# Corner weights of a bilinear gather: a multiply with broadcast weights and two pair sums on VectorE, in place of scale and accumulate tap by tap on two engines

## The chip, the cores and the metric

The kernel runs on one core of one Trainium2 chip. The metric is the device time of one launch in microseconds (us). The core has five engines with queues of their own: PE (TensorE), DVE (VectorE), ACT (ScalarE), POOL (GpSimd) and SP (SyncE). Each runs its instructions in the order in which the program put them. SP issues plain DMAs; POOL issues the indirect ones, which gather rows of a DRAM tensor by a list of indices.

## The reference

Four layers run over four samples of 96 channels and 128 x 128 pixels, all in float32, each layer added to its input. Layer 2 is a deformable 3 x 3 convolution, and only its sampling is touched here:

```python
offset = _conv(x, offset_w, offset_b)
mask = jax.nn.sigmoid(_conv(x, mask_w, mask_b))
...
for k in range(K * K):
    i, j = (k // K, k % K)
    dy = offset[:, 2 * k]
    dx = offset[:, 2 * k + 1]
    py = base_y[None, :, None] + i * DIL + dy
    px = base_x[None, None, :] + j * DIL + dx
    samp = _bilinear(x, py, px) * mask[:, k][:, None]
    out = out + jnp.einsum('bchw,oc->bohw', samp, weight[:, :, i, j])
```

`_bilinear` takes, for every pixel, the four corners around (py, px) and adds them with the weights (1-wy)(1-wx), (1-wy)wx, wy(1-wx) and wy wx. So every pixel and each of the nine taps has four weights (here already multiplied by the mask) and four vectors of 96 channels, and the sample is the weighted sum of the four vectors. The other layers are a selective scan along the pixels (layer 0), convolutions with two-dimensional transforms (layer 1), and a transform, a large selective scan with 16 states and the inverse transform (layer 3).

## The kernel before

**Stages and lanes.** The samples overlap. First the front of sample 0 runs (layers 0 and 1 and the preparation of layer 2). Then for each sample b there is a stage with two lanes side by side: the "back" of sample b (the gather of layer 2, then the head and the forward transform of layer 3), and the front of sample b+1 with the inverse transform of sample b-1. After it come the scans of layer 3 of sample b, by themselves. For the last sample there is no next front; the lane beside it has only the inverse transform of the sample before, which is done early, so that most of that gather runs alone. There are four gathers: three beside a front, one alone.

**Order.** Inside a two-lane stage the program is recorded first: a planner (`Program`, line 238) keeps a cost per operation (`cost`, line 368), measures each lane once for due times, and issues the operations of both lanes engine by engine, by the earliest start and then by the due time. `InOrder` (line 56) keeps that order on the chip. All instructions of these stages are issued at line 66, a helper, so groups are told apart by their tiles. A tile's name stands in the profile without digits: `l2_g` is `l_g`, `l2_sm` is `l_sm`, `l2_v` (the weights) is `l_v`.

**The data.** `offsets` (line 1247) writes three DRAM tensors: `quad_d`, which holds for each pixel the 4 x 96 values of its four corners; `idx_d`, the row of `quad_d` for each pixel and tap; and `w4_d`, the four weights for each pixel and tap. On its way it runs DVE operations on tiles `l_off`, `l_p`, `l_rd`, `l_w`. The front lane's layer 0 runs the scan `l_h` on DVE with its products `l_du` on POOL and `l_ct` on DVE.

**The gather** (`gather`, line 1421) goes row by row over the 128 rows of the image; partition w holds pixel w of the row. For a row, POOL issues nine indirect DMAs, one a tap, each of 128 rows of 384 floats, into the tile `l2_g` [128, 9, 384]. There are four such tiles beside the other lane, six in the last stage (`room`, line 1410). In the turns of the next row, `weigh(row, 0)` is recorded for taps 0 to 4 and `weigh(row, 1)` for taps 5 to 8; both read the weights from `l2_v`. For each tap ACT scales corner 0 into `l2_sm` and corner 2 into `l2_part`; DVE adds corner 1 times its weight to the first and corner 3 times its weight to the second. One DVE sum for each half then adds `l2_part` to `l2_sm`. A row's `l2_sm` [128, 9, 96] is then transposed by PE (`turn`), copied to SBUF by ACT (`keep`) and multiplied with the convolution's weights by PE (`finish`). Every four rows DVE adds bias and input (`l_x<-l_pc`) and takes statistics.

Of the kernel before, what the change touches and what calls it, by code (L numbers as in the profile page):

```python
# [23 lines left out]
F32 = mybir.dt.float32  # L24
F32R = mybir.dt.float32r
I32 = mybir.dt.int32
AF = mybir.ActivationFunctionType
ALU = mybir.AluOpType
# [4 lines left out]
C, H, W = 96, 128, 128  # L33
# [492 lines left out]
class Net:  # L526
# [894 lines left out]
    def gather(self, T, wp, wb, ps, rows, sums, kept, lag, slack):  # L1421

        nc, a = self.nc, self.a
        T.x3, T.st3 = self.plane("x3"), self.stats_tile()
        KC = 7

        wk = wp.tile([128, KC, C], F32, name="l2_wk")
        for k in range(9):
            c = 0
            while c < C:  # L1430
                at = k * C + c
                n = min(C - c, 128 - at % 128)
                nc.sync.dma_start(
                    out=wk[at % 128 : at % 128 + n, at // 128, :], in_=a["l2_wT"][c : c + n, k, :]
                )
                c += n
        bk = self.load(wp, a["l2_b"], [C, 1], "l2_bk")
        gts, sms, work = {}, {}, {}

        def fetch(g):  # L1440
            idx = wb.tile([128, 36], I32, name="l2_i", tag="i", bufs=3)
            nc.sync.dma_start(out=idx, in_=T.idx_d[:, 36 * g : 36 * (g + 1)])
            w4 = wb.tile([128, 144], F32, name="l2_v", tag="v", bufs=3)
            nc.sync.dma_start(out=w4, in_=T.w4_d[:, 144 * g : 144 * (g + 1)])
            xc = self.load(wb, T.x2[:, g * CH : (g + 1) * CH], [C, CH], "l2_x", 3)
            work[g] = SimpleNamespace(idx=idx, w4=w4, xc=xc)

        def weigh(row, m):


            if m == 0:
                sms[row] = wb.tile([128, 9, C], F32, name="l2_sm", tag="sm", bufs=sums)
            taps = slice(5 * m, 5 + 4 * m)
            part = wb.tile([128, 5, C], F32, name="l2_part", tag="part")
            sm = sms[row][:, taps]
            g4 = gts[row][:, taps].rearrange("p k (q c) -> p k q c", c=C)
            for k in range(5 - m):
                at = 36 * (row % 4) + 4 * (5 * m + k)
                w = [work[row // 4].w4[:, at + q : at + q + 1] for q in range(4)]
                for q, out in ((0, sm), (2, part)):  # L1460
                    nc.scalar.activation(out[:, k, :], g4[:, k, q, :], AF.Copy, scale=w[q])
                    nc.vector.scalar_tensor_tensor(
                        out[:, k, :], g4[:, k, q + 1, :], w[q + 1], out[:, k, :], ALU.mult, ALU.add
                    )
            nc.vector.tensor_tensor(sm, sm, part[:, : 5 - m], ALU.add)

        def turn(p, c):
            v = units[p, c] = SimpleNamespace(ks=[k for k in (2 * c, 2 * c + 1) if k < KC])
            v.pt = ps.tile([128, 2, 2, W], F32, name="l2_pt2", tag="t")
            for i, k in enumerate(v.ks):  # L1470
                n = min(128, 9 * C - 128 * k)
                for r in range(2):
                    flat = sms[2 * p + r].rearrange("p k c -> p (k c)")
                    nc.tensor.transpose(v.pt[:n, i, r, :], flat[:, 128 * k : 128 * k + n], self.ident)

        def keep(p, c):
            v = units[p, c]
            v.sT = wb.tile([128, 2, 2, W], F32, name="l2_sT", tag="sT", bufs=kept)
            n = min(128, 9 * C - 128 * v.ks[-1])
            nc.scalar.copy(v.sT[:n, : len(v.ks)], v.pt[:n, : len(v.ks)])  # L1480

        def finish(p, c):
            g, h = divmod(p, 2)
            w, v = work[g], units.pop((p, c))
            if h == 0 and c == 0:
                w.pc = ps.tile([128, CH], F32, name="l2_pc", tag="pc", bufs=1)[:C]
            for i, k in enumerate(v.ks):
                n = min(128, 9 * C - 128 * k)
                nc.tensor.matmul(
                    out=w.pc[:, 2 * W * h : 2 * W * (h + 1)], lhsT=wk[:n, k, :],  # L1490
                    rhs=v.sT[:n, i].rearrange("c r w -> c (r w)"),
                    start=k == 0, stop=k == KC - 1,
                )
            if h == 1 and c == 3:
                nc.vector.scalar_tensor_tensor(w.xc, w.pc, bk, w.xc, ALU.add, ALU.add)
                nc.vector.bn_stats(T.st3[:, g, :], w.xc)
                nc.sync.dma_start(out=T.x3[:, g * CH : (g + 1) * CH], in_=w.xc)

        fetch(0)
        units = {}  # L1500
        self.program.slack = slack
        at = (0, 4, 9, 13)
        for row in range(H + 6):
            if row % 4 == 2 and row // 4 + 1 < H // 4:
                fetch(row // 4 + 1)
            for k in range(9):
                if row < H:
                    if k == 0:
                        gts[row] = wb.tile([128, 9, 4 * C], F32, name="l2_g", tag="g", bufs=rows)
                    i = (row % 4) * 9 + k  # L1510
                    nc.gpsimd.indirect_dma_start(
                        out=gts[row][:, k, :],
                        out_offset=None,
                        in_=T.quad_d[:],
                        in_offset=work[row // 4].idx[:, i : i + 1],
                    )
                if k in (2, 5) and 0 <= row - 1 < H:
                    weigh(row - 1, k // 5)
                for late, step in ((0, turn), (lag, keep), (lag + 4, finish)):
                    p, m = divmod(9 * row + k - 27 - late, 18)  # L1520
                    if 0 <= p < H // 2 and m in at:
                        step(p, at.index(m))
                yield
        self.program.slack = 0.0
# [926 lines left out]
```

## Time and profile before

Median 14923.91 us of 3 runs (14919.98 to 14983.37). The profiled execution took 14956.1 us, and its span from the first to the last instruction is 14954.0 us.

| stretch, us from the start | what runs | POOL busy of it |
|---|---|---|
| 0 to 1318 | front of sample 0 | |
| 1318 to 3190 | gather of sample 0, beside front of sample 1 | 1270.70 |
| 4817 to 6676 | gather of sample 1, beside front of sample 2 | 1270.59 |
| 8345 to 10195 | gather of sample 2, beside front of sample 3 | 1264.33 |
| 11826 to 13292 | gather of sample 3, most of it alone | 1114.65 |
| between and behind | layer 3's head, transform and scans of each sample | |

Each gather issues 1152 indirect DMAs. A line of the profile's groups reads: line, engine, operation, out<-in by tiles, partitions x elements, count | busy us, mean ns of one | idle time of the engine just before them and what ended most of it. "issue" is time in which the engine waited for nothing that the profile shows. Lines in order of time read: start, us, engine, line, operation, tiles, [idle before <- what ended it].

### The profile page before, as it was taken

Reading aid. Unit: us, or ns where it says so; the run is one execution under the profiler, and the core shown is the slowest. Engines: PE = TensorE matmul, PEld = TensorE weight load, DVE = VectorE, ACT = ScalarE, POOL = GpSimd, SP = SyncE. Lnnn points to the kernel's source line nnn. Section 1 sums busy time; section 2 is a strip of 40 time slices with the busy share of each in tenths; the row PEclk is TensorE's granted clock in tenths of the full one; section 3 lists DMA queues with packets and bytes.
Section 4 is the critical chain, followed back from the end, with each engine's and each line's share of the span. In section 5 each row is a group of like instructions: output and inputs, shape, how many; then the busy total and the mean of one; then the engine's idle time right before and its main releaser. Section 6 shows DMA issues by size and latency. Waiting matters only on the chain. (4 is left out here: it accounts for less than half of the span.)

```text
span 14954.0 us, 175601 instructions
## 1 busy us (share of the span) xinstructions
PE 12275.2 (82%) x48112; PEld 5769.1 (39%) x48112; DVE 11311.0 (76%) x21823; ACT 8881.9 (59%) x21508; POOL 10357.0 (69%) x7904
## 2 busy tenths in 40 slices
PE   7897787879998978878999878887999744459998
PEld 3353344343333434443333334534333422233334
DVE  4625686678998587677999678667999765558997
ACT  3614675556665586555666467555666465546664
POOL 2103747748998755765999774774999877758997
PEclk9998898979999988978999989888999855569999
DMA  6445658766666758875666766876666755556676
GB/s 163 135 131 187 185 168 249 233 205 177 188 196 192 243 169 225 236 221 162 194 189 193 222 202 176 255 237 186 192 189 196 213 171 168 166 153 184 187 199 193
DMA packets 1313229, 2890.16 MB, mean 193 GB/s; under 512 B 281008, under 2 KB 767600, under 8 KB 1197936
## 3 DMA queue, kind: packets, MB, share of 16 engines
q1 hardware_dynamic: 1013872, 1972.56, 45.8%
q0 software_dynamic: 298368, 906.38, 20.5%
q8 instruction: 381, 6.24, 0.2%
q14 instruction: 608, 4.98, 0.1%
HBM read 2455.55 MB, written 422.58 MB: 192 GB/s over the span
## 5 line engine op out<-in xcount | busy, mean ns | idle before, releaser
L66 POOL DMA_INDIRECT l_g<-quad_d,l_i x4608 | 4664.4, 1012 | 2516.9 <-issue 1330.6
L66 POOL TENSOR_TENSOR l_hc<-l_h,l_cl 128x1024 f32<-128x1024 f32 x1536 | 3608.5, 2361 | 288.6 <-DVE l_h L66 264.1
L66 PE MATMUL l_py<-l_hc,ident 128*128 128x512 f32 x6144 | 3073.9, 611 | 181.2 <-POOL l_hc L66 177.9
L66 DVE TENSOR_TENSOR_SCAN l_h<-l_dA,l_carry,l_dB 128x512 f32<-128x512 f32 x2304 | 2861.4, 1265 | 1.7
L66 ACT ACTIVATE l_dA<-l_dl,l_al 128x512 f32<-128x512 f32 x2304 | 1637.4, 718 | 1111.6 <-DVE l_h L66 1102.6
L66 DVE SCALAR_TENSOR_TENSOR l_sm<-l_g,l_v,l_sm 128x96 f32<-128x96 f32 x4608 | 1480.5, 322 | 1039.4 <-ACT l_sm L66 1004.6
L66 ACT ACTIVATE l_sm<-l_g,l_v 128x96 f32<-128x96 f32 x4608 | 1680.1, 369 | 646.8 <-DMA l_g<-quad_d,l_i 612.3
L66 ACT ACTIVATE l_part<-l_g,l_v 128x96 f32<-128x96 f32 x4608 | 1656.6, 364 | 213.3 <-DVE l_sm L66 213.1
L66 PEld LDWEIGHTS l_py<-l_hc,ident 128*128 128x128 f32 x6144 | 1135.2, 192 | 1348.3 <-issue 828.0
L66 PE MATMUL l_pc<-l_sT,l_wk 128*96 128x256 f32 (+1 forms) x3584 | 1238.3, 470 | 449.9 <-ACT l_sT L66 447.4
L66 DVE TENSOR_TENSOR l_dB<-l_du,l_pB 128x512 f32<-128x512 f32 x2304 | 1492.2, 677 | 48.7 <-POOL l_du L66 27.7
L66 PE MATMUL l_pB<-l_bc,pick 128*128 128x512 f32 x2304 | 1402.1, 637 | 136.1 <-DVE l_dB L66 122.1
L66 DVE SCALAR_TENSOR_TENSOR l_part<-l_g,l_v,l_part 128x96 f32<-128x96 f32 x4608 | 1477.8, 321 | 43.8 <-ACT l_part L66 43.1
L66 PE MATMUL l_pt<-ident,l_sm 128*128 128x128 f32 (+1 forms) x3584 | 793.7, 326 | 750.7 <-DVE l_sm L66 746.2
L66 POOL TENSOR_TENSOR l_dP<-l_du,l_cl 128x512 f32<-128x512 f32 x768 | 978.1, 1274 | 100.9 <-DMA l_cl<-bc_d 71.6
L66 DVE TENSOR_TENSOR_SCAN l_h<-l_dQ,l_carry,l_dP 128x512 f32<-128x512 f32 x768 | 971.1, 1264 | 58.1 <-POOL l_dP L66 54.7
L66 PEld LDWEIGHTS l_pc<-l_sT,l_wk 128*96 128x96 f32 (+1 forms) x3584 | 643.2, 199 | 962.4 <-ACT l_sT L66 552.2
L66 PEld LDWEIGHTS l_pt<-ident,l_sm 128*128 128x128 f32 (+1 forms) x3584 | 521.7, 164 | 1140.1 <-DVE l_sm L66 874.7
L66 ACT COPY l_sT<-l_pt 128x512 f32<-128x512 f32 (+1 forms) x1024 | 522.3, 522 | 626.8 <-PE l_pt L66 625.5
L66 POOL TENSOR_TENSOR l_du<-l_du,l_dl 96x512 f32<-96x512 f32 x256 | 339.9, 1328 | 792.8 <-DVE l_dl L66 482.5
L66 PE MATMUL l_pc<-rows,l_wc 96*32 96x508 f32 (+3 forms) x6912 | 841.7, 612 | 46.7 <-DVE rows L66 46.7
L66 PEld LDWEIGHTS l_pB<-l_bc,pick 128*128 128x128 f32 x2304 | 438.5, 191 | 1062.2 <-DVE l_dB L66 834.5
(274 smaller groups left out, 19887.2 us busy)
## 6 DMA issues: line engine op xcount, KB each, us to landing
l_cl<-bc_d SPq DMA_DIRECT2D x512, 1280.0 KB
l_cl<-bc_d SPq DMA_DIRECT2D x512, 640.0 KB
quad_d<-l_qt SPq DMA_DIRECT2D x124, 768.0 KB
l_g<-quad_d,l_i POOLq DMA_INDIRECT x4608
x<-l_x SPq DMA_DIRECT2D x352, 192.0 KB
l_uc<-u_d SPq DMA_DIRECT2D x256, 192.0 KB
l_x<-x SPq DMA_DIRECT2D x224, 192.0 KB
l_xs<-x SPq DMA_DIRECT2D x116, 256.0 KB
```

The lines of the kernel that those rows point to most:

```text
L66: ins = op(*args, **kw).ins
```

## The change

`weigh` weighs a half row at once. One DVE operation multiplies the gathered tile in place, all taps of the half, four corners and 96 channels (128 x 1920 or 128 x 1536 elements), by the weights, each of which is repeated over 96 channels by a stride of zero. A second adds the last two corners to the first two (128 x 960 or 128 x 768), in place too. A third adds the two halves of that into `l2_sm` (128 x 480 or 128 x 384). ACT has no part in it any more, and the tile `l2_part` is gone. The indirect DMAs, their tiles and the number of these, the transposes and the rest are written as before; the planner works out the order of the stage anew from the new operations.

```diff
             taps = slice(5 * m, 5 + 4 * m)
-            part = wb.tile([128, 5, C], F32, name="l2_part", tag="part")
-            sm = sms[row][:, taps]
-            g4 = gts[row][:, taps].rearrange("p k (q c) -> p k q c", c=C)
-            for k in range(5 - m):
-                at = 36 * (row % 4) + 4 * (5 * m + k)
-                w = [work[row // 4].w4[:, at + q : at + q + 1] for q in range(4)]
-                for q, out in ((0, sm), (2, part)):
-                    nc.scalar.activation(out[:, k, :], g4[:, k, q, :], AF.Copy, scale=w[q])
-                    nc.vector.scalar_tensor_tensor(
-                        out[:, k, :], g4[:, k, q + 1, :], w[q + 1], out[:, k, :], ALU.mult, ALU.add
-                    )
-            nc.vector.tensor_tensor(sm, sm, part[:, : 5 - m], ALU.add)
+            n = 5 - m
+            at = 36 * (row % 4) + 20 * m
+            w = work[row // 4].w4[:, at : at + 4 * n].rearrange("p (k q) -> p k q", q=4)
+            g4 = gts[row][:, taps]
+            by_q = g4.rearrange("p k (q c) -> p k q c", c=C)
+            nc.vector.tensor_tensor(by_q, by_q, w.unsqueeze(3).to_broadcast([128, n, 4, C]), ALU.mult)
+            nc.vector.tensor_tensor(g4[:, :, : 2 * C], g4[:, :, : 2 * C], g4[:, :, 2 * C :], ALU.add)
+            nc.vector.tensor_tensor(sms[row][:, taps], g4[:, :, :C], g4[:, :, C : 2 * C], ALU.add)
```

## The prediction

> **What bounds the kernel now.** I read the page first, then the busy times by stretch, then the groups of single engines inside stretches, then the order of time at a few places.
>
> The page, first two lines of part 1 and the first of part 5:
>
> ```profile
> span 14954.0 us, 175601 instructions
> PE 12275.2 (82%) x48112; PEld 5769.1 (39%) x48112; DVE 11311.0 (76%) x21823; ACT 8881.9 (59%) x21508; POOL 10357.0 (69%) x7904
> L66 POOL DMA_INDIRECT l_g<-quad_d,l_i x4608 | 4664.4, 1012 | 2516.9 <-issue 1330.6
> ```
>
> No engine is full, since the span is a row of stages with different limits. Busy time by stretch (time, then PE, PEld, DVE, ACT, POOL, each with its count, then the clock, the DMA share and GB/s) shows three kinds: a gather beside the other lane, the gather of the last sample alone, and the layer-3 scans.
>
> ```profile
> 2500.00:2750.00 250.00, 193.57 (x1322) 96.06 (x1326) 142.65 (x463) 127.73 (x446) 183.86 (x188) 0.90 0.76 222
> 4250.00:4500.00 250.00, 238.51 (x600) 97.20 (x599) 244.00 (x269) 172.88 (x325) 237.16 (x132) 1.00 0.69 197
> 12250.00:12500.00 250.00, 107.67 (x308) 65.94 (x308) 148.53 (x452) 142.67 (x440) 189.98 (x198) 0.56 0.57 166
> ```
>
> The change touches the first and third kind. In both POOL does little but indirect DMAs, at nearly one rate. POOL's groups from 12000 to 13250 us, and from 2260 to 3190 us (count, then busy, mean ns, idle before it):
>
> ```profile
> L66 POOL DMA_INDIRECT l_g<-quad_d,l_i x985 | 951.2, 966 | 300.1 <-issue 279.4 <-DVE l_sm L66 12.5 <-DVE l_part L66 6.4
> ...
> L66 POOL DMA_INDIRECT l_g<-quad_d,l_i x675 | 685.3, 1015 | 244.2 <-issue 184.6 <-DVE l_part L66 41.1 <-DMA l_g<-quad_d,l_i 11.5
> ```
>
> An undisturbed one takes 0.946 us (the median) and the next starts 0.304 us later: 1.25 us each, 11.25 us for a row of nine. Alone, 985 fill the 1250 us (1.27 each); beside the other lane 675 fill 930 (1.38). So the gather stages are set by how fast POOL can issue gathers. The exception is the layer-0 scan inside each of the first three stages (1740 to 2260 us and its like), where POOL waits for DVE. The same group in the other five stretches outside it counts 304, 333, 679, 316 and 690; with the 675 that is 2997 DMAs or 333 rows. The last stage has 128 rows, the three layer-0 stretches 51.
>
> What lengthens a DMA is seen in the order of time (start, us, engine):
>
> ```profile
> 10048.24 0.84 DVE L66 TENSOR_TENSOR l_off<-l_ot 128x656 f32<-128x656 f32 x1
> 10048.33 1.56 POOL L66 DMA_INDIRECT l_g<-quad_d,l_i  x1 [0.30 <-DVE l_ot L66]
> 10049.11 0.84 DVE L66 TENSOR_TENSOR l_off<-l_off,l_ot 128x656 f32<-128x656 f32 x1
> ...
> 9054.46 1.27 DVE L66 TENSOR_TENSOR_SCAN l_h<-l_dA,l_e,l_du 96x512 f32<-96x512 f32 x1
> 9054.64 2.49 POOL L66 DMA_INDIRECT l_g<-quad_d,l_i  x1 [0.30 <-issue]
> 9055.65 0.66 DVE L66 TENSOR_TENSOR l_ct<-l_ct,l_z 96x512 f32<-96x512 f32 x1
> ```
>
> The first began inside a DVE operation with both inputs in SBUF and ended 0.82 us after that operation (49.90 against 49.08), though a second one, dependent on the first, ran from 0.03 us later. The second sat through a scan and an independent product that followed without a gap, and ended 0.82 us after the product (57.13 against 56.31). So a gather passes one point, 0.946 - 0.82 = 0.13 us after its start, only while no such DVE operation runs; the 0.03 us gap before a dependent operation lets it through. The 96-element operations of before are too short to matter: 0.966 against 0.946.
>
> **The change part by part.** *Removed:* ACT's 2 x 4608 scalings (1680.1 + 1656.6 us) and DVE's 9216 accumulations and 1024 sums (1480.5 + 1477.8 + 637.1 = 3595 us, 7.02 a row). ACT's 6.5 us a row hid beside POOL's 11.4, so it is worth nothing by itself. *Added:* six DVE operations a row, all with two SBUF inputs. Their durations come from the same operation at two widths alone, with one broadcast row as a check:
>
> ```profile
> L66 DVE TENSOR_TENSOR l_sm<-l_sm,l_part 128x480 f32<-128x480 f32 x112 | 73.7, 658 | 3.8
> L66 DVE TENSOR_TENSOR l_sm<-l_sm,l_part 128x384 f32<-128x384 f32 x113 | 63.0, 558 | 3.9
> ...
> L66 DVE TENSOR_TENSOR pick<-ident 128x768 fp32r<-128x768 f32 x8 | 7.2, 943 | 0.0
> ```
>
> 96 more elements cost 100 ns, so 1.042 each on 158. Products of 1920 and 1536: 2.158 and 1.758 us; sums of 960, 480, 768 and 384: 1.158, 0.658, 0.958, 0.558. Together 7.25 us a row. The row of 768, whose inputs are both broadcast in the innermost place, took 0.943 where this gives 0.958: repeating an element is not slow. The upper bound is the four-apart write, l_w<-l_w,l_w at 144 elements, 0.503 us: (503 - 158)/144 = 2.4 ns each; the lower is 1.042. I take the lower. DVE's own sum is then +0.2 us a row, hidden under POOL.
>
> The product waits for all of its five or four taps where ACT began with each, so the sums, the transposes on PE behind them and the release of the gather's buffer come later, by up to the 3.97 or 3.27 us of a half's three operations. Alone PE works 656.95 of 1464 us (11826 to 13290) and has the room; a buffer is wanted again six rows on, or four beside the other lane, 45 us at 11.4 a row. I cost it at nothing; were that cover gone, POOL would wait 3 us a row more.
>
> *The wait it makes on POOL, last stage.* A scaling on ACT starts 2.1 us after its gather ends (12499.65 + 0.95, ACT at 12502.70); the product starts so after its last tap. From the end of that DMA, the following ones reach their point at 0.43, 1.68 and 2.93 us. The first product holds DVE from 2.1 to 4.26: the third waits 1.33. The next reaches it 1.25 later; by then the first sum (0.03 to 1.19) is over and the second (1.23 to 1.88) has just begun: 0.63. For the second product, 2.1 + 1.76 - 2.93 = 0.93, and the sum behind it (1.03 to 1.58) costs 0.33. In all 3.22 us a row, less the 9 x 0.02 = 0.18 that the old operations cost: 3.04 x 128 = 389 us. Whether the 0.63 falls hangs on 0.02 us; without it and the 0.33 it is 2.26 - 0.18 = 2.08 a row, 266 us.
>
> *The first three stages.* There the weighing runs some two rows behind the gather, so the phase is anyone's. A product longer than the 1.25 us period stops some gather for its length less 0.625 on average: 1.53 and 1.13; behind it 0.63 and 0.33 as above: 3.62. The old ones cost between 0.18 and (1.015 - 0.946) x 9 = 0.62 a row; I take 0.3. 3.3 x 333 rows = 1105 us. Lower bound, sums slipping through: 2.66 - 0.62 = 2.04, 679 us. Upper, both halves back to back so that a sum and the next product leave no gap: 1.53 + (0.63 + 1.67) + 0.33 = 4.16, less 0.18: 1325 us.
>
> *Given back.* In the six stretches POOL also lost about 200 us to waits beyond its 0.304 us gaps (39 in the one shown: 244.2 - 675 x 0.304), for gather buffers that ACT and DVE freed late. With ACT out of the chain and a slower gather I take half, 100; bounds 0 and 200.
>
> *The layer-0 stretches.* Their 51 rows are set by DVE (454 busy of 520 us from 1740 to 2260): +0.2 us a row, POOL's l_du products held by longer DVE work against fewer waits for ACT. I take 0, bounds -100 and +100. In the built order the gathers stand beside l_du at the same rows (34 to 51) in both kernels. The layer-3 scans run none of this: 0.
>
> The sum is 389 + 1105 - 100 = +1394 on the span of 14954.0 (its execution took 14956.1, 0.2% above the median of 14923.91): 16350, or some **16320 us** against the median.
>
> The page "SBUF — State Buffer" of the Trainium skill, section "Who interferes with whom", says that a Vector instruction with two SBUF inputs blocks a GpSimd instruction that reads SBUF, for its whole length. The same section also says that a probe saw tensor_copy stall such DMAs and tensor_tensor not, inferring that descriptor generation needs the write side alone. By that second sentence the change would stall nothing and the sum would be a small gain; the 1.56 us above agrees with the first.
>
> **Rivals.** *A: no stall; POOL runs free.* If a broadcast operand kept the product off what POOL needs, only the old stalls and waits would go: -(0.18 x 128 + 0.3 x 333) - 100 = -223, **14700 us**, faster. Deciding point: a mean of the indirect DMA under 1.012 us. Against it: every kind of two-input SBUF operation in the trace stalls the gather. *B: nothing moves.* The gather waits less often than I count and the stalls cancel the gains: 14920. Against it: the products are longer than a gather period, so some gather must meet each. *C: the product is slow.* At 2.4 ns an element the products take 4.77 and 3.84 us, the row 11.9 us of DVE and the stalls 4.14 + 0.63 + 3.22 + 0.33 = 8.3; 8.1 x 128 + 8.0 x 333 - 100 + 4.9 x 51 = +3850, **18800**. Against it: the broadcast row.
>
> **How the numbers follow.** Forecast 0.88, A 0.04, B 0.03, C 0.05. The forecast's own bounds: 266 + 679 - 200 - 100 = +645 and 389 + 1325 + 100 = +1814, so 15570 to 16740 on the median. All at the low end at once is unlikely, so the range is 15700 to 16740. A change under 0.5% (75 us) can't be told from none: faster 0.04, same 0.03, slower 0.93.
>
> **What would show it.** Right: DMA_INDIRECT's mean near 1.3 to 1.4 us; rows near 14.5 us alone (11.4 before) and 15 beside the other lane; products at 2.16 and 1.76; ACT down by 3337 us, DVE about level; the scans' stages unchanged, the last stage's gather some 1850 us long instead of 1465. Wrong: a mean that stays near 1.0, or products off these durations. If POOL's gathers lengthen but the stages do not, the gather was not the bound where I took it to be.

## The result and the profile after

The changed kernel takes 16075.42 us (median of 4 runs, 16062.81 to 16086.24) against 14943.7 us for the kernel before (median of 4, 14919.98 to 14983.37): 1.0752 times the time, interval 1.0732 to 1.0772. The profiled execution took 16062.81 us. From its page, the first two lines of part 1 and the line of the indirect DMAs in part 5:

```profile
span 16060.1 us, 157166 instructions
PE 12449.2 (78%) x48112; PEld 5852.9 (36%) x48112; DVE 11950.9 (74%) x14655; ACT 6412.9 (40%) x12293; POOL 11689.3 (73%) x7904
...
L66 POOL DMA_INDIRECT l_g<-quad_d,l_i x4608 | 5911.8, 1283 | 2317.5 <-issue 1329.9
```

ACT is busy for 2469 us less and DVE for 640 more, and neither is where the time went. (By the busy times of their groups ACT lost 3337 and DVE gained some 150; the old operations of 96 elements overlapped on their engines, DVE's lasting 0.31 us and starting 0.23 us apart, and the busy time counts an overlap once.) POOL issues the same 4608 gathers; one takes 1.283 us in the mean instead of 1.012, which adds 5911.8 - 4664.4 = 1247 us to POOL's busy time, and the span is 1106 us longer. The new operations (groups of DVE, shapes kept apart: count, then busy, mean ns, idle before):

```profile
L66 DVE TENSOR_TENSOR l_g<-l_g,l_v 128x1920 f32<-128x1920 f32 x512 | 1106.0, 2160 | 621.2 <-DMA l_g<-quad_d,l_i 616.1 <-issue 4.7
L66 DVE TENSOR_TENSOR l_g<-l_g,l_v 128x1536 f32<-128x1536 f32 x512 | 898.0, 1754 | 331.2 <-DMA l_g<-quad_d,l_i 328.1 <-issue 2.9
L66 DVE TENSOR_TENSOR l_g<-l_g 128x960 f32<-128x960 f32 x512 | 597.8, 1168 | 13.2
L66 DVE TENSOR_TENSOR l_g<-l_g 128x768 f32<-128x768 f32 x512 | 492.8, 962 | 13.4
L66 DVE TENSOR_TENSOR l_sm<-l_g 128x480 f32<-128x480 f32 x512 | 354.5, 692 | 15.0 <-PE l_pt L66 0.9
L66 DVE TENSOR_TENSOR l_sm<-l_g 128x384 f32<-128x384 f32 x512 | 292.2, 571 | 14.7
```

Busy time by stretch, at three places that answer to those of before (a gather beside the other lane, a stretch of layer-3 scans, the last gather):

```profile
2500.00:2750.00 250.00, 189.10 (x809) 128.28 (x810) 162.09 (x215) 52.26 (x141) 202.16 (x158) 0.82 0.70 202
4650.00:4900.00 250.00, 240.55 (x594) 98.34 (x593) 243.40 (x268) 172.81 (x324) 236.01 (x130) 0.99 0.69 197
13000.00:13250.00 250.00, 84.13 (x252) 55.05 (x252) 137.33 (x118) 18.22 (x36) 200.95 (x162) 0.58 0.46 135
```

In the last gather POOL is busy for 200.95 us of 250, more than before (189.98), and issues fewer instructions (162 for 198). It is longer held, not idle. From the start of the first gather to the end of the last, the four gather stages were 1871.2, 1858.2, 1849.7 and 1465.3 us long and are now 2129.3, 2134.7, 2129.3 and 1791.2: +258, +277, +280 and +326, in all +1140. Everything between them together went down by some 34.

A row of the last gather shows how a gather is held (order of time: start, us, engine, line, operation):

```profile
13196.07 2.16 DVE L66 TENSOR_TENSOR l_g<-l_g,l_v 128x1920 f32<-128x1920 f32 x1 [2.91 <-DMA l_g<-quad_d,l_i]
13196.66 2.39 POOL L66 DMA_INDIRECT l_g<-quad_d,l_i  x1 [0.30 <-issue]
13198.27 1.16 DVE L66 TENSOR_TENSOR l_g<-l_g 128x960 f32<-128x960 f32 x1
13199.35 0.95 POOL L66 DMA_INDIRECT l_g<-quad_d,l_i  x1 [0.30 <-issue]
13199.46 0.66 DVE L66 TENSOR_TENSOR l_sm<-l_g 128x480 f32<-128x480 f32 x1
...
13202.44 1.76 DVE L66 TENSOR_TENSOR l_g<-l_g,l_v 128x1536 f32<-128x1536 f32 x1 [2.32 <-DMA l_g<-quad_d,l_i]
13203.11 1.91 POOL L66 DMA_INDIRECT l_g<-quad_d,l_i  x1 [0.30 <-issue]
13204.23 0.96 DVE L66 TENSOR_TENSOR l_g<-l_g 128x768 f32<-128x768 f32 x1
13205.22 0.56 DVE L66 TENSOR_TENSOR l_sm<-l_g 128x384 f32<-128x384 f32 x1
13205.32 1.27 POOL L66 DMA_INDIRECT l_g<-quad_d,l_i  x1 [0.30 <-issue]
```

The first gather began inside the product, which ended at 13198.23; the gather ended 0.82 us after that, at 13199.05. The second reached its point, 0.13 us after its start, at 13199.48, when the narrow sum had run for 0.02 us, and was not held at all (0.95). The third and fourth were held by the second product (it ended at 13204.20, the gather at 13205.02) and by the last sum (13205.78 and 13206.59). So a row has three holds, where the prediction counted four. It is no matter of one row: of the last gather's DMAs, 250 reached their point well inside a product (0.18 us or more after its start, 0.10 or more before its end), and all 250 ended 0.82 us after it, to within 0.05.

### The profile page after: what moved, and what is told of

It is laid out like the page before. It is cut to its first block, busy times and chain, and to the rows that moved or that the text cites. A ratio compares the mean times of both kernels' runs of the same rounds, so it can differ in the third digit from the quotient of the medians.

```text
span 16060.1 us, 157166 instructions
## 1 busy us (share of the span) xinstructions
PE 12449.2 (78%) x48112; PEld 5852.9 (36%) x48112; DVE 11950.9 (74%) x14655; ACT 6412.9 (40%) x12293; POOL 11689.3 (73%) x7904
## 5 line engine op out<-in xcount | busy, mean ns | idle before, releaser
L66 POOL DMA_INDIRECT l_g<-quad_d,l_i x4608 | 5911.8, 1283 | 2317.5 <-issue 1329.9
L66 DVE TENSOR_TENSOR l_g<-l_g,l_v 128x1920 f32<-128x1920 f32 (+1 forms) x1024 | 2004.0, 1957 | 952.4 <-DMA l_g<-quad_d,l_i 944.2
L66 DVE TENSOR_TENSOR l_g<-l_g 128x960 f32<-128x960 f32 (+1 forms) x1024 | 1090.6, 1065 | 26.6
L66 POOL TENSOR_TENSOR l_du<-l_du,l_dl 96x512 f32<-96x512 f32 x256 | 425.4, 1663 | 795.4 <-DVE l_dl L66 495.8
L66 PE MATMUL l_p<-rows,l_c 96*32 96x508 f32 (+3 forms) x6912 | 823.3, 622 | 85.2 <-DMA rows<-cat_d 85.2
L66 PE MATMUL l_pu<-l_xq,l_wc 96*64 96x512 f32 (+1 forms) x2048 | 791.6, 615 | 16.5 <-ACT l_xq L66 13.6
```

The source lines that it names most:

```text
L66: ins = op(*args, **kw).ins
```

## The experiments

Twelve runs follow. The measure of most is a row of the last gather, where nothing else disturbs: the time from the start of a row's first gather to that of the next row's, median over the rows of the stage. It was 11.39 us before and is 14.04 after. Ten of the runs fell on chips (1 to 4 on chip 6, 5 to 8 on chip 5, 9 on chip 2, 12 on chip 7) on which the kernel before takes over 16.5 ms. Experiments 8 to 12 ask about that; in the others only rows, holds and differences within one chip are read. Runs 1 to 4 were timed once each (16222.98, 16246.91, 16335.83 and 16355.41 us), with the kernel before (16554.21) but no changed kernel beside them.

**1. The weights in PSUM, last gather only.** The product then has one input in SBUF and one in PSUM.

```diff
+        vp = ps.tile([128, 3, 144], F32, name="l2_vp", tag="vp", bufs=1) if rows == 6 else None
...
+            if rows == 6:
+                nc.scalar.copy(vp[:, g % 3], w4)
+                w4 = vp[:, g % 3]
```

> In the last gather alone the four weights are copied by ACT into PSUM and the product reads them there, so that it has one SBUF input in place of two; its length, its place and what it waits for stay. Theory (a gather is held while DVE runs an operation with two SBUF inputs): the products hold nothing any more, only the sums do. First product from 2.2 to 4.36 us after the fifth tap's DMA; the reads at 2.93 and 4.18 pass; the one at 5.43 waits 0.12 for the wide sum; in the second half the one at 4.18 waits 0.77. Row 11.25 + 0.9 = 12.1 us (11.7 to 12.5) against 14.0 in the changed kernel, last gather some 1555 us against 1791. Rival (the gather is late because a half row is weighed as a whole, by late buffers or by DVE's working time): row stays at 14.0, gather 1790. The first three gathers stay as they are under both.

The row took 12.07 us. (The last gather as a whole took 1708.9 us where some 1555 was expected; ten rows of 19 us and more make 284 of them, and the last experiments come back to these.) The product kept its length but not its place: it starts 20.9 us after its last tap's DMA in the median, where it was 2.3. So the row alone could be a matter of place, and what decides is which operations hold:

```profile
13699.35 2.15 DVE L66 TENSOR_TENSOR l_g<-l_g,l_vp 128x1920 f32<-128x1920 f32 x1
13700.55 0.95 POOL L66 DMA_INDIRECT l_g<-quad_d,l_i  x1 [0.30 <-issue]
13701.53 1.16 DVE L66 TENSOR_TENSOR l_g<-l_g 128x960 f32<-128x960 f32 x1
13701.80 1.70 POOL L66 DMA_INDIRECT l_g<-quad_d,l_i  x1 [0.30 <-issue]
```

The second line began in the middle of the product and took its 0.95; the fourth was held by the sum, whose inputs are both in SBUF, and ended 0.81 us after it. Counted over this last gather as above, 280 DMAs reached their point inside a product, none of them was held, and all took at most 1.00 us; of the 103 inside the wide sum of the first half every one was held to its end. In experiment 6 a product held none of 1012. So it is the two SBUF inputs of these operations that hold a gather, and not their length, their place or their writing into the gathered tile.

**2. The product corner by corner, last gather.** Four operations of 480 or 384 elements, none dependent on another.

```diff
-            nc.vector.tensor_tensor(by_q, by_q, w.unsqueeze(3).to_broadcast([128, n, 4, C]), ALU.mult)
+            step = 1 if rows == 6 else 4
+            for q in range(0, 4, step):
+                at_q = slice(q, q + step)
+                nc.vector.tensor_tensor(
+                    by_q[:, :, at_q], by_q[:, :, at_q],
+                    w[:, :, at_q].unsqueeze(3).to_broadcast([128, n, step, C]), ALU.mult,
+                )
```

> In the last gather alone the product is made corner by corner: four independent operations of 480 or 384 elements back to back, none of which waits for the one before. Theory (only a gap between DVE operations lets a gather pass, and independent ones leave none): the chain of four, about 4 x 0.58 + 0.08 = 2.4 us (2.0 in the second half), holds the gather like one long product: waits 1.66 + 1.26 + 0.33, row 14.5 us (14.0 to 14.8). Rival (each instruction holds it by itself, so that short ones cost little): no wait over 0.66 us, row at most 12.5.

12.69 us: the theory (operations back to back hold as one) fell. The view in order of time shows four merged in one line, and a gather among them:

```profile
13705.87 1.97 DVE L66 TENSOR_TENSOR l_g<-l_g,l_v 128x384 f32<-128x384 f32 x4 [1.14 <-DMA l_g<-quad_d,l_i]
13706.48 1.24 POOL L66 DMA_INDIRECT l_g<-quad_d,l_i  x1 [0.31 <-issue]
```

The gather ended at 13707.72, 0.82 us after 13706.90, which is the end of the second of the four (each is 0.55 us long and begins some 0.08 us before the one ahead of it ends). It did not wait for the fourth, at 13707.84. Of 149 gathers that reached their point 0.2 us or more inside one of the four, 148 ended 0.82 us after that same one. Each tensor_tensor holds by itself, and between two independent ones a gather gets through. The rival's row, at most 12.5 us, was missed too, by 0.19. The scan followed at once by a product, shown in the prediction, did hold through; two tensor_tensors do not.

**3. Tap by tap, last gather.** For each tap a product of 384 and sums of 192 and 96 elements; 10.6 us of DVE a row.

```diff
+            step = 1 if rows == 6 else n
+            for k in range(0, n, step):
+                t = slice(k, k + step)
+                o = slice(5 * m + k, 5 * m + k + step)
...
```

> In the last gather alone each tap has its own product (384), sum (192) and sum (96), the second and third each waiting for the one before. DVE's time a row rises from 7.25 to 9 x (0.558 + 0.358 + 0.258) = 10.6 us. Theory (what counts is how long DVE goes without a gap): a read waits at most 0.56 us, mostly 0.1, row 11.6 to 12.6 us, last gather 1490 to 1610 against 1791, although DVE works 45% more. Rival (the loss goes with DVE's working time, or with the time that two-input operations run): 2.75 x 10.6 / 7.25 = 4.0 us a row, row 15.3, slower than the changed kernel.

12.03 us, inside the theory's range for the row; the whole stage, 1724.0 us, is not inside its 1490 to 1610, with 281 us in 14 rows of 19 us and more. Short operations, though more of them and more DVE time, hold less. The row's cost goes with the length of the single operation.

**4. The first wide sum shorter.** It leaves out 16 of 192 columns (1.074 us for 1.158), so that the gather which passed in the seam meets the narrow sum further in.

```diff
-            nc.vector.tensor_tensor(g4[:, :, : 2 * C], g4[:, :, : 2 * C], g4[:, :, 2 * C :], ALU.add)
+            c = 2 * C - (16 if rows == 6 and m == 0 else 0)
+            nc.vector.tensor_tensor(g4[:, :, :c], g4[:, :, :c], g4[:, :, 2 * C : 2 * C + c], ALU.add)
```

> In the last gather alone the wide sum of the first half leaves out 16 of its 192 columns (part of the computation is left out), 80 of 960 elements, so that it ends 0.083 us earlier and the narrow sum behind it begins 1.14 instead of 1.23 us after the product's end, before the next gather's read at 1.25. Theory (the second stop of 0.63 us was missed by 0.02 us of timing): the read now comes 0.1 us into the narrow sum and waits 0.55 us, row 14.55 instead of 14.0, last gather some 1860 us: less work, slower. Rival (a narrow sum never holds the gather there, or its first 0.1 us still lets it pass): 13.9 to 14.0.

14.07 us: the theory fell again.

```profile
13705.25 1.08 DVE L66 TENSOR_TENSOR l_g<-l_g 128x880 f32<-128x880 f32 x1
13706.34 0.95 POOL L66 DMA_INDIRECT l_g<-quad_d,l_i  x1 [0.30 <-issue]
13706.36 0.67 DVE L66 TENSOR_TENSOR l_sm<-l_g 128x480 f32<-128x480 f32 x1
```

The gather reaches its point, 0.13 us after its start, 0.11 us into the narrow sum, and still takes 0.95; the sum is some 0.016 us longer instead (0.673 for 0.657 in the median). In the row of the changed kernel above, one that reached it 0.23 us into the last sum was held. The hold sets in between those. Counted in four traces with these operations (the changed kernel, 4, 8 and 11): of 1733 gathers whose point came less than 0.12 us after a tensor_tensor's start 1667 took their usual time, and of 1848 whose point came 0.18 to 0.4 us after it none did.

**5. ACT's load put back.** Both scalings of each tap, into a tile that nothing reads.

```diff
+            part = wb.tile([128, 5, C], F32, name="l2_part", tag="part")
+            for k in range(n):
+                for q in (0, 2):
+                    nc.scalar.activation(part[:, k, :], by_q[:, k, q, :], AF.Copy, scale=w[:, k, q : q + 1])
```

> The changed kernel, with ACT's old scalings of corners 0 and 2 kept beside it as idle work into a scratch tile that nobody reads (18 a row, 6.6 us of ACT). Theory (ACT's relief was worth nearly nothing): last gather's rows stay at 14.0 (to 14.3), rows beside the other lane at 14.3 to 14.8, the whole 0 to 150 us over the changed kernel. Rival (the relief of ACT gave back a good part of what the held gathers cost): rows beside the other lane over 15.3, some 350 us or more on the whole.

16283.49 us on chip 5, against 16324.83 for the changed kernel on that chip (experiment 8). By the profiled spans (16304.2 and 16308.7 us) that is +20 in the first three gathers, -93 in the last and some +69 outside them. So the scalings cost something beside the other lane, where rows took 14.9 to 15.2 us for 14.6 to 14.8, and the last gather hides it: its row fell to 13.03. Neither row nor the whole lies in the range that the theory gave, and the rival's (some 350 us or more) did not come either. In the last gather the product now waits for ACT's reads, so it starts 2.97 us after its last tap's DMA instead of 2.32, at another place in the gathers' rhythm, and holds less (1.09 and 0.59 us a row for 1.41 and 0.99).

**6. The weights in PSUM in all four gathers.** To make room in PSUM, beside the other lane the transposes get one buffer instead of two, and another tile three instead of four.

```diff
-        room = (5, 6, 6, 5, 12, 8.0) if alone else (2, 4, 5, 3, 4, 3.0)
+        room = (4, 6, 6, 5, 12, 8.0) if alone else (1, 4, 5, 3, 3, 3.0)
```

> The weights stand in PSUM for the product in all four gathers (ACT copies them once every four rows); to make room for them the transposes have one PSUM buffer instead of two beside the other lane, four instead of five in the last gather. Theory: the products hold no gather any more (1.36 and 0.98 us a row beside the other lane in the changed kernel), the sums hold somewhat more than now (0.45 to some 0.8): rows of 12.2 to 13.0 instead of 14.3, last gather's rows 12.1; the whole some 700 to 900 us under the changed kernel, still 200 to 400 over the kernel before. Rival (beside the other lane the loss has another cause: order, buffers or DVE's time): rows there stay over 14, the whole only some 250 us under the changed kernel.

**7. The product corner by corner in all four.** The edit of 2, with step 1 throughout.

> The product corner by corner, four independent operations back to back, in all four gathers. After the second experiment the theory reads: each instruction holds the gather by itself, up to its own end, and independent ones with a tensor as second operand let it pass between them. Then rows beside the other lane 12.6 to 13.6 instead of 14.3, last gather 12.7, the whole 400 to 700 us under the changed kernel, though DVE has 6 x 0.1 us or so more to do in a row. Rival (beside the other lane, where the queue on DVE is never empty, no gap opens): rows there as in the changed kernel, the whole 150 us under it.

| chip 5 | time, us | mean of an indirect DMA beside the other lane / alone, ns | rows of 19 us and more, us a gather (first three) |
|---|---|---|---|
| changed kernel (8) | 16324.83 | 1276 to 1281 / 1248 | 620 to 657 |
| PSUM in all (6) | 16654.18 | 1039 to 1049 / 1032 | 1003 to 1094 |
| four products in all (7) | 16294.98 | 1151 to 1172 / 1103 | 713 to 919 |

Both held the gathers less, as the theory said, beside the other lane too, and both missed the time: 700 to 900 and 400 to 700 us under the changed kernel were expected, 329 over it and 30 under it came. The usual row beside the other lane did fall, from 14.6 to 14.8 us to 13.6 (6) and 13.7 to 14.2 (7), though not into the ranges expected. What was won on each gather came back in a few very long rows, in which POOL waits for a buffer (for DVE's `l_sm`: 1133 us in the long rows of the first three gathers in 6, 691 in 7, 352 in 8). In 6 the single transpose buffer is a cause that can't be separated from the next point; 7 has no such excuse.

**8, 9. The changed kernel, and the kernel before, without an edit.**

> The changed kernel once more on the chip of the other three, as their measure. All theories: 1.075 of the kernel before, rows of 14.0 and 14.3 us.

> The kernel before, unchanged, with a profile on the same kind of chip job as the last eight, where its time was given as some 16560 us against the 14924 of the first measurement, while the changed kernel took 16325 against 16075. If the chip is slower for it, the profile shows where the 1600 us are (longer rows beside the other lane, longer scans, or a lower clock); if it runs in some 14950 to 15150 us, the other figure belongs to something else than this kernel and no ratio is taken from it.

On chip 5 the changed kernel took 16324.83 us and the kernel before 16580.04 (ratio 0.9851, interval 0.9825 to 0.9877): the sign is the other one. On chip 2 the kernel before took 16588.57 as a kernel of its own and 16553.97 as the one compared with (1.001, 0.9986 to 1.0034). So it is not the kernel that differs. Each chip stands for one series of runs, so whether it is the chip or the time of measuring can't be told apart; "chip" means both from here on. By the spans, the kernel before was 1650 us longer on chip 2 than in the first measurement, 1526 of them in the four gathers, and the changed kernel 249 us longer on chip 5, 228 of them in the gathers. The clock is not needed for it: the changed kernel was granted 0.866 in the first measurement and 0.864 on chip 5. On the page of 9:

```profile
span 16603.7 us, 175601 instructions
...
L66 POOL DMA_INDIRECT l_g<-quad_d,l_i x4608 | 4718.2, 1024 | 3958.8 <-DVE l_part L66 1626.0
L66 ACT COPY l_sT<-l_pt 128x512 f32<-128x512 f32 (+1 forms) x1024 | 530.4, 528 | 1912.2 <-remote 1203.0
```

A gather takes 1.024 us as ever (1.012 in the first measurement), but POOL is idle ahead of gathers for 3959 us instead of 2517, 1626 of it waiting for DVE (201.9 before), and ACT waits 1203 us for something that the profile can't name ("remote"). One such place:

```profile
13814.16 0.95 POOL L66 DMA_INDIRECT l_g<-quad_d,l_i  x1 [0.30 <-issue]
13822.50 0.59 ACT L66 COPY l_sT<-l_pt 128x512 f32<-128x512 f32 x1 [29.81 <-remote]
...
13823.14 2.02 PE L66 MATMUL l_pc<-l_sT,l_wk 128*96 128x256 f32 x4 [23.15 <-ACT l_sT L66]
...
13823.39 0.32 DVE L66 SCALAR_TENSOR_TENSOR l_sm<-l_g,l_v,l_sm 128x96 f32<-128x96 f32 x1 [20.22 <-ACT l_sm L66]
...
13827.34 1.15 POOL L66 DMA_INDIRECT l_g<-quad_d,l_i  x1 [12.24 <-DVE l_part L66]
```

PE and DVE wait for ACT, POOL for DVE, and ACT for PE's transposes, which by their records had ended at 13799.99. The trace also keeps when semaphores were raised, and there PE's five last raises, by records of 13786.54 to 13799.57, stand at 13822.42 to 13823.27; ACT went on 0.02 us after the first. Counted over whole traces (an instruction that raises its engine's semaphore, and the first raise recorded after its end):

```
                      PE: over 3 us late    ACT                 DVE
before, first chip    0 of 10939            2 of 19908          0 of 20343
before, chip 2 (9)    725 of 10939          877 of 19908        1051 of 20343
changed, chip 5 (8)   358 of 10779          287 of 10826        303 of 13742
changed, chip 9 (11)  1 of 10779            1 of 10826          0 of 13742
```

Where a raise is missing from the record, the next one counts in its place, so the counts are upper bounds. POOL's raises are on time everywhere. On chip 2 fewer raises are recorded, too (15853 for ACT, where 19908 instructions raise). In the two stretches where raises and raising instructions were counted apart they agree outside the gathers (1641 of 1641 for ACT between the third and the fourth gather) and not inside (1601 of 2508 in the last gather).

**10, 11. VectorE tied to ScalarE tap by tap; the changed kernel again.** 10 adds to 5 a copy of one element after each scaling, and its scalings are 48 columns wide.

```diff
+            part = wb.tile([128, 5, 2, C // 2], F32, name="l2_part", tag="part")
+            mark = wb.tile([128, 10], F32, name="l2_mark", tag="mark")
+            for k in range(n):
+                for q in (0, 1):
+                    nc.scalar.activation(part[:, k, q, :], by_q[:, k, 2 * q, : C // 2], AF.Copy, scale=w[:, k, 2 * q : 2 * q + 1])
+                    nc.vector.tensor_copy(mark[:, 2 * k + q : 2 * k + q + 1], part[:, k, q, :1])
```

> The changed kernel with 18 scalings a row on ScalarE again, of 48 columns each, and after each of them an instruction of VectorE that copies one element of what it wrote into a tile that nothing reads: VectorE is tied to ScalarE tap by tap as it was before, at some 18 x 0.16 = 2.9 us of VectorE a row, which has 4 us to spare in a row of 14. The question is why the kernel before takes 16.55 ms on chips 2, 5 and 6 and 14.94 ms in the first measurement, with rows of some 20 us in which VectorE, ScalarE and TensorE stand still together. Theory (on these chips an engine learns late that another is done, so every wait of one engine on another in the gathers costs, and the kernel before had 18 more of them a row): against the changed kernel of the same call (e11) +500 to +1200 us, the rows of 19 us and more sum to some 900 a gather instead of 640, and rows of 20 us appear in the last gather. Rival (the number of waits between engines is not it): within +150 of e11, sums of the long rows as in e11.

> The changed kernel without any edit, beside e10 on the same chip. Both: 16300 to 16350 on a chip where the kernel before takes 16550 (as e8 was), 16060 to 16090 on one where it takes 14940.

These fell on chip 9, where the kernel before took 14947.15 us, as in the first measurement. The changed kernel took 16095.4: 1.0766 times that (1.0746 to 1.0786), the result once more (the number of the first measurement's chip is not on record, so this may be the same one). 10 took 16176.41, 1.0821 times (1.08 to 1.0843). Without late raises on this chip it says nothing on them, though it lies within the rival's +150, but it prices ACT and the bond to ACT: 81 us more than 11, made of +119 in the three gathers beside the other lane (2151.1, 2189.1 and 2187.7 us against 2144.2, 2131.1 and 2133.9), -71 in the last (1719.0 against 1790.5, the shifted product as in 5) and the rest outside.

**12. The kernel of 7 again,** hoped to fall on such a chip.

> The kernel of e7 once more (the product of every half made corner by corner, four independent instructions of 480 or 384 elements), hoped to fall on a chip like that of e11, where no late signals were seen. Theory (on such a chip the time follows the stops of the gathers' reads): a read is stopped some 0.13 us less in the mean than in e11 beside the other lane (1.16 for 1.29 us in e7's own trace), 9 x 0.13 = 1.2 us a row on 384 rows and 14.0 - 12.7 = 1.3 on 128, so -450 to -630 us against e11's 16095, of which a fifth may be given back: 15450 to 15750. Rival (what e7 showed is the kernel's own: the long rows grow as the stops go): 16030 to 16100. On a chip where the kernel before takes 16550, 16290 as in e7, which tells nothing new.

It fell on chip 7, where the kernel before took 16717.7: 16478.14 us, 0.9848 times (0.9807 to 0.9889). What four products are worth on a chip like 9 was not measured.

The lengths of the last gather over all runs do show how those chips differ:

| last gather | median row, us | length, us |
|---|---|---|
| before / changed, first chip | 11.39 / 14.04 | 1465.3 / 1791.2 |
| before (9), chip 2 | 11.66 | 1712.6 |
| PSUM (1), chip 6; (6), chip 5 | 12.07; 12.13 | 1708.9; 1705.9 |
| four products (2), chip 6; (7), chip 5; (12), chip 7 | 12.69; 12.68; 12.70 | 1689.5; 1693.3; 1715.4 |
| tap by tap (3), chip 6 | 12.03 | 1724.0 |
| ACT's load (5), chip 5 | 13.03 | 1713.3 |
| shorter sum (4), chip 6 | 14.07 | 1801.3 |
| changed (8), chip 5 | 14.06 | 1806.6 |

On the chips 2, 5, 6 and 7 no kernel's last gather is shorter than 1689 us, some 1.47 us for each of the 1152 indirect DMAs, whatever its usual row; the ones that could go faster lose the difference in rows of 19 us and more, and those that are slower anyway lose almost nothing. This looks like a limit on the rate, which hides most of what the holds cost there; if it is one, that is how the change can lose 1130 us on one chip and win 250 on another. What makes it is open. That raises land late while gathers run fast is seen; whether this is its cause, an effect of something else, or has to do with the recording, no run here told. Every time here comes with a span of the same execution, so none shows the kernels unrecorded. No kernel was measured faster than the kernel before on a chip where that takes 14.95 ms.

## Why the prediction was right

The forecast was right in sign, in what holds a gather and in range: 16320 against 16075 us, with the span put at +1394 where it was +1106. Where a hold begins it had wrong. The holds were put 391 us too high, and 103 us came back from terms that were put too low or at nothing, which is luck. (Its "first and third kind" of stretch are those of its three lines, the two gathers, and not those of its sentence.) Step by step, on the first chip:

- *Durations.* 2.158, 1.758, 1.158, 0.958, 0.658 and 0.558 us were predicted; 2.160, 1.754, 1.168, 0.962, 0.692 and 0.571 measured. Repeating weights by a stride of zero costs nothing. With that rival C, the slow product, fell. A, that nothing is held, fell by the mean of the indirect DMA (1.283 us, not under 1.012), and B, that nothing moves, by the time itself.
- *The mechanism.* Shown by the counts: a product that reads both inputs from SBUF held 250 of 250 gathers in the last stage, one that reads its weights from PSUM none of 280 there (1) and none of 1012 in all four (6). Of the two sentences of the Trainium skill set against each other ("SBUF — State Buffer", "Who interferes with whom"), the one on two SBUF inputs agrees with 2.39 us for a gather inside a product, and the one beside it, that an operation with at most one SBUF input does not contend outside the two-port modes, with the 0.95 of experiment 1. Whether the page's inference on descriptor generation is wrong is not shown: the indirect DMA also reads its indices, `l_i`, from a tile, and no run tells which of the two is held.
- *The last stage: mis-sized by one term.* 1.33, 0.63, 0.93 and 0.33 us a row were predicted, less 0.18 for the old operations: 389 us. Counted in the trace by which operation's end plus 0.82 us a gather's end falls on: 1.42, 0, 1.02 and 0.33, in all 2.78, less 0.19. Three terms stand and the 0.63 is not there. The row went up by 2.65 us, x 128 = 339, and the stage by 326. The timing came as predicted, with the gather's point 0.02 us into the narrow sum in the median. What failed is the step from there to a hold: the prediction let an operation hold from its first moment on, and a gather that comes 0.11 us into it still passes (experiment 4). Its lower bound for this stage, 266 us, dropped the 0.33 along with the 0.63, and that one is real.
- *The first three: the same term.* 3.62 us of holds a row, less 0.3, were predicted: 3.3 x 333 = 1105. Counted: 1.36 and 0.98 for the products (1.53 and 1.13 predicted), 0.23 for the last sum (0.33), 0.20 for the wide sums and none for the sum behind the first (0.63 for the sums of the first half), and some 0.15 for the rest; 2.92, less 0.59 that the kernel before had, makes 2.34 x 333 = 777. The 0.63 failed for the same reason as above and is 210 of the 328 us by which the term was too high; the old holds, put at 0.3 and near the upper end of their own bounds at 0.59, are 97 more. That a hold passes to the next operation where no gap lies between, which made the upper bound of 1325, did not come for tensor_tensors either (experiment 2).
- *Given back.* 100 was predicted. The three gathers grew by 814, of which 108 lie in layer 0's stretches, so 706 of the 777 are left: 71. In experiment 10, with ACT back in the chain, these three cost 119 more, but 10 also adds 18 short DVE copies a row.
- *Layer 0's stretches.* 0 was predicted, with bounds of 100 either way; from 406, 508 and 502 us they grew to 445, 539 and 539 (rows 34 to 46 of the first gather, 36 to 53 of the others), +108 together, just past the bound. By the rows that stand beside POOL's `l_du` in both traces (33 to 45 and 39 to 51) it is +132, and 95 given back, so these two terms are known to some 25 us. What made it was not tried.

In all 1394 - 63 - 328 (holds that did not come, and old ones that went) + 29 (less given back) + 108 (layer 0) - 34 (between the gathers) = 1106. Of the rows, 14.5 us alone and 15 beside the other lane were predicted; medians of 14.04 and 14.5 were measured.

## What to carry to other kernels

When an indirect DMA's issue sets the pace, count which VectorE operations read two SBUF inputs while it runs: the length of each matters, not their sum, and 10.6 us a row in short pieces held the gathers less than 7.3 in long ones. Moving one input to PSUM frees the gathers, and splitting the operation frees them in part; what either is worth in time was not measured where the kernel before takes 14.95 ms. Relieving an engine that was not the bound gave back little here, 71 to 95 us. The sign of a few per cent belongs to the chips on which it was measured: here it was +7.5% and +7.7% in two series of runs and -1.5% in a third.

## What the runs showed of the hardware

- A hold does not begin with the operation: a gather whose point comes 0.11 us after a tensor_tensor's start passes, at 0.016 us to that operation, and one that comes at 0.23 us is held to its end.
- Two SBUF tensors are not the only thing that holds. In the trace of before, 38 gathers reached their point inside a long TENSOR_SCALAR (`rows`, 2304 or 2176 elements, and `l_xs`, 2048), which reads one SBUF tensor and took 1.37 us for 2048 elements, where the line of the tensor_tensors gives 158 + 2048 x 1.042 = 2292 ns; 34 were held to its end, and none took its usual time. BATCH_NORM_STATS2, with one SBUF input too, let 76 of 82 through.
- A later start can make a shorter row: with the product pushed back by ScalarE's reads, the row fell from 14.06 to 13.03 us (5) and from 14.07 to 12.98 (10). The kernel of 10 as a whole was 81 us slower all the same. To place the product on purpose was not tried.
- Of six series of runs, two had the kernel before at some 14.95 ms (the first and chip 9) and four at 16.55 to 16.72, with the same instructions, and, where it was profiled, a mean of 1.012 us (first chip) and 1.024 us (chip 2) for a gather.
